# A graph-attention kernel: the row of target scores by a DRAM table and a broadcast load instead of TensorE transposes

## The chip, the cores and the metric

The kernel runs on one core of a Trainium2 chip. The core has TensorE (PE in the profile, its weight loads as PEld), VectorE (DVE), ScalarE (ACT), GpSimd (POOL) and SyncE (SP), which here issues nearly all ordinary transfers; sixteen DMA engines move the data. The metric is the device time of the whole kernel in microseconds, the median of several runs. One further execution was recorded by the hardware profiler, and all durations come from it.

## The reference

Four graph-attention layers run one after the other on 4096 nodes with 256 features. The adjacency matrix is 4096 × 4096, fixed and sparse, and denser towards the low node numbers. Layers 0 to 3 have 1, 1, 4 and 2 heads. (The two heads of layer 3 are the positive and the negative attention.) Each layer normalises the rows of x, projects them, scores every connected pair by a target part plus a source part, and takes the softmax over a target's sources. Cut to one layer with one head:

```python
h = jnp.maximum(_layernorm(x), 0.0) @ W
e = (h @ a1)[:, None] + (h @ a2)[None, :]      # target i, source j
e = jnp.where(e > 0, e, 0.2 * e)               # leaky relu
e = jnp.where(adj > 0, e, MASK_VAL)
x = x + elu(softmax(e, axis=1) @ h)
```

Layer 0 has a bias and no elu, layer 2 has four heads of 64 features and no elu, and layer 3 combines two attentions, the second with the signs of the scores turned, and returns the elu of their sum without adding x.

## The kernel before

The kernel uses that exp(leaky(s + t)) is the larger of exp(s + t) and exp(0.2(s + t)). With factors that cancel in the softmax taken out, the weight of source j for target i is max(grow[i], factor[j]) times the mask, where grow[i] = exp(0.8 s[i]). In layer 2 ScalarE makes two of the four heads of some units, in the form relu(grow · factor − 1), to be completed by VectorE; for these heads grow is the exp of −0.8 s. So everywhere one needs, for a block of targets, a tile in which every partition holds the same row: grow of these targets along the free dimension. How this row comes onto all partitions is what the change is about.

**Tiles and units.** The nodes are 32 tiles of 128. Per layer, `node_rows` (L683) normalises two tiles, transposes them (s_tp, L716), and calls `project` (L739), whose matmuls (s_pj, L748) give the features, two factors of the source, and the target score s. ScalarE writes the score of tile T to `L.s[:, T, :]` (L766 in layer 0, L773 in the others): one node per partition, one column per head. The features with their factors go to a DRAM table by SP (L727 in layer 0, four tiles at once; L729 in the others, each tile).

The attention itself is done by units (class `Unit`, L981). A dense unit holds four target tiles (512 targets) and runs over all 32 source tiles; there are 4, 2, 1 and 1 dense blocks in layers 0 to 3 (in layer 3 a block's two heads are two units that share their grow). A listed unit holds one target tile (128 targets) and runs over 4 source tiles kept in SBUF (pre) and then over 6 to 13 chunks of 128 sources from its own list, which GpSimd gathers from the DRAM table with an indirect transfer (s_gg, L1231). There are 16, 24, 28 and 28 listed units.

**grow.** `target_rows` (L954) makes it. For each head and target tile TensorE transposes the column of s, broadcast to 128 × 128, by the identity (s_sT, L967): the result in PSUM has the row of s on every partition. ScalarE takes the exp of it, scaled, into the SBUF tile s_grow (L973). The PSUM tiles come from a pool of two buffers that s_tp, s_pj and others share. For listed units and layer 0's dense units grow has two buffers; it is reused when the last weighing of the unit before the last is done.

**Order.** The steps of the units stand in a plan, and `run` (L1194) walks through it. At step p it fetches step p, begins step p−2 (ScalarE's relu in layer 2, L1019), weighs step p−3 (VectorE, L1033 and L1042, into s_p) and multiplies step p−6 (TensorE, s_acc at L1071, in layer 2 s_accm at L1096). Before these it prepares, that is makes grow of, a unit whose first step is four steps ahead, if all its scores are there:

```python
if p + 4 < n and plan[p + 4][1] == 0 and plan[p + 4][0].is_ready():
    plan[p + 4][0].prepare()
```

If they are not there yet, grow is made when the unit is first fetched. Between steps, parts of the work of finishing a tile and of projecting it for the next layer are pumped out of a queue by a clock of costs. In layer 0 the listed units are mixed with the dense steps, while the adjacency is loaded (s_raw, L1306, 512 KB each), turned into masks and stored. In layers 1 and 2 listed units are mixed with the dense steps until these are used up, and then follow each other alone; in layer 3 they run through all the dense steps. The program order is not final: a list scheduler reorders the instructions of TensorE, ScalarE, VectorE and SP. GpSimd keeps the written order. Each engine then runs its instructions in order, and so does SP, the queue of the stores and loads.

In layer 1 and later, some gathered rows carry the masks of the list along, which ScalarE copies out (mlist, L1056) ahead of their use.

The path through `list_layers` is the one that runs; `dense_layers` is a fallback behind a flag, and is not touched.

Of the kernel before, what the change touches and what calls it, by code (L numbers as in the profile page):

```python
# [8 lines left out]
F32 = mybir.dt.float32  # L9
# [3 lines left out]
AF = mybir.ActivationFunctionType  # L13
# [4 lines left out]
P = 128  # L18
N = 4096
# [7 lines left out]
SLOPE = 0.2  # L27
# [440 lines left out]
LH = (1, 1, HEADS, 2)  # L468
# [11 lines left out]
def list_layers(ctx: ExitStack, tc: tile.TileContext, a: dict, out: bass.AP, flag):  # L480

    nc = tc.nc
# [6 lines left out]
    dram = ctx.enter_context(tc.tile_pool(name="s_dram", bufs=1, space=bass.MemoryType.DRAM))  # L489
    ps_acc = ctx.enter_context(tc.tile_pool(name="s_acc", bufs=6, space=PSUM))  # L490
    ps_mm = ctx.enter_context(tc.tile_pool(name="s_mm", bufs=2, space=PSUM))


    ident = const.tile([P, P], F32, name="s_ident")
# [28 lines left out]
        if b not in MASKS_IN  # L523
    }

    def table_rows(t, jt):

        r0 = jt // CH * CH * P
        r0 += 1 if r0 >= HALF else 0
        return t[r0 : r0 + CH * P, :].rearrange("(p k) d -> p k d", k=CH)  # L530

    def feature_rows(l, jt):
        return table_rows(table[l], jt)[:, :, FRONT[l] : FRONT[l] + GW[l]]
# [149 lines left out]
    def node_rows(L, T0):  # L683


        u = f"{L.l}_{T0}"
        tiles = (T0, T0 + 1)
        while any(stored[T] < L.l - 1 for T in tiles) or not L.made:
            yield
        mv = small.tile([P, 2, 2], F32, name=f"s_mv_{u}", tag="mv")  # L690
        for k, T in enumerate(tiles):
            st6 = small.tile([P, 6], F32, name=f"s_st6_{u}_{k}", tag="st6")
            nc.vector.bn_stats(st6, x[:, T, :])
            nc.vector.bn_aggr(mv[:, k, :], st6)
            yield
        r = small.tile([P, 3, 2], F32, name=f"s_r_{u}", tag="r")
        nc.scalar.activation(r[:, 0], mv[:, :, 1], AF.Ln, bias=eps)
        nc.scalar.activation(r[:, 0], r[:, 0], AF.Exp, scale=-0.5)
        zs = []
        for k, T in enumerate(tiles):  # L700
            z = rows.tile([P, D], F32, name=f"s_z_{u}_{k}", tag="z", bufs=4)
            (nc.gpsimd if L.l == 0 else nc.vector).tensor_scalar(z, x[:, T, :], mv[:, k, 0:1], 0.0, op0=ALU.subtract, op1=ALU.max)
            zs.append(z)
        if L.bias is not None:
            for T in tiles:
                nc.gpsimd.tensor_add(x[:, T, :], x[:, T, :], L.bias[:, 0:D])
        yield 1.5

        nc.vector.scalar_tensor_tensor(r[:, 1], mv[:, :, 1], EPS, r[:, 0], op0=ALU.add, op1=ALU.mult)
        nc.vector.scalar_tensor_tensor(r[:, 1], r[:, 1], -0.5, r[:, 0], op0=ALU.mult, op1=ALU.mult)  # L710
        nc.vector.scalar_tensor_tensor(r[:, 2], r[:, 1], 1.5, r[:, 0], op0=ALU.add, op1=ALU.mult)
        hTs = []
        for k, T in enumerate(tiles):
            tp = ps_mm.tile([P, 2, P], F32, name=f"s_tp_{u}_{k}", tag="mm")
            for c in range(2):
                nc.tensor.transpose(tp[:, c, :], zs[k][:, c * P : (c + 1) * P], ident)  # L716
            hT = rows.tile([P, 2, P], F32, name=f"s_hT_{u}_{k}", tag="hT")
            nc.scalar.copy(hT, tp)  # L718
            hTs.append(hT)
            yield  # L720
        yield 1.5
        for k, T in enumerate(tiles):
            g = L.rows(T)
            yield from project(L, T, g, hTs[k], r[:, 2, k : k + 1])
            L.ready[T] = True
            if L.l == 0 and T % CH == CH - 1:
                nc.sync.dma_start(feature_rows(L.l, T), L.g[:, T - CH + 1 : T + 1, :])  # L727
            elif L.l > 0:
                nc.sync.dma_start(feature_rows(L.l, T)[:, T % CH, :], g)  # L729
# [9 lines left out]
    def project(L, T, g, hT, r):  # L739
        l, H, n = L.l, L.H, L.part  # L740
        u = f"{l}_{T}"
        re = small.tile([P, H], F32, name=f"s_re_{u}", tag=f"re{H}")
        parts = g.rearrange("p (h n) -> p h n", h=H)
        for k in range(2 if l == 3 else 1):
            cols = D if k else D + 3 * H
            ps = ps_mm.tile([P, cols], F32, name=f"s_pj_{u}_{k}", tag="mm")
            for c in range(2):
                nc.tensor.matmul(  # L748
                    ps,
                    lhsT=hT[:, c, :],  # L750
                    rhs=L.w[:, c, k * (D + 6) : k * (D + 6) + cols],
                    start=(c == 0),
                    stop=(c == 1),
                )
            if k == 0:
                t = ps[:, D + H : D + 3 * H]
                if L.bias is not None:
                    for i in range(2):
                        nc.scalar.activation(
                            g[:, D + i : D + i + 1],  # L760
                            t[:, i : i + 1],
                            AF.Exp,
                            scale=r,
                            bias=L.bias[:, D + 1 + i : D + 2 + i],
                        )
                    nc.scalar.activation(  # L766
                        L.s[:, T, :], ps[:, D : D + H], AF.Identity, scale=r, bias=L.bias[:, D : D + 1]
                    )
                else:
                    nc.scalar.activation(  # L770
                        parts[:, :, n - 2 : n], t.rearrange("p (h k) -> p h k", h=H), AF.Exp, scale=r
                    )
                    nc.scalar.activation(L.s[:, T, :], ps[:, D : D + H], AF.Copy, scale=r)  # L773
                nc.scalar.activation(re, parts[:, :, n - 2], AF.Copy, scale=r)
            if l == 2:
                nc.vector.tensor_tensor(
                    parts[:, :, 0:DH],
                    ps[:, 0:D].rearrange("p (h o) -> p h o", h=H),
                    re.unsqueeze(2).to_broadcast([P, H, DH]),
                    op=ALU.mult,  # L780
                )
            else:
                nc.scalar.activation(parts[:, k, 0:D], ps[:, 0:D], AF.Copy, scale=re[:, k : k + 1])
            yield
# [169 lines left out]
    def target_rows(L, T0, nt, big, nact):  # L954


        w = nt * P
        grow = (L.big if big else L.pool).tile(
            [P, L.H, w], F32, name=f"s_grow_{L.l}_{T0}", tag=big or "grow", bufs=None if big == "growb" else 2
        )  # L960
        per = max(1, 512 // w)
        for h0 in range(0, L.H, per):
            hs = range(h0, min(L.H, h0 + per))
            ps = ps_mm.tile([P, len(hs), nt, P], F32, name=f"s_sT_{L.l}_{T0}_{h0}", tag="mm")
            for h in hs:
                for it in range(nt):
                    nc.tensor.transpose(  # L967
                        ps[:, h - h0, it, :], L.s[:, T0 + it, h : h + 1].to_broadcast([P, P]), ident
                    )
            cut = min(max(L.H - nact, hs.start), hs.stop)  # L970
            for h1, h2, scale in ((hs.start, cut, 1.0 - SLOPE), (cut, hs.stop, SLOPE - 1.0)):
                if h1 < h2:
                    nc.scalar.activation(  # L973
                        grow[:, h1:h2, :],
                        ps[:, h1 - h0 : h2 - h0].rearrange("p h a b -> p h (a b)"),
                        AF.Exp,
                        scale=scale,
                    )
        return grow

    class Unit:  # L981
# [212 lines left out]
    def run(plan):  # L1194

        n = len(plan)
        for p in range(n + LEAD[3]):
            if p + 4 < n and plan[p + 4][1] == 0 and plan[p + 4][0].is_ready():
                plan[p + 4][0].prepare()
            for lead, stage in zip(LEAD, (Unit.fetch, Unit.begin, Unit.weigh, Unit.multiply)):  # L1200
                if 0 <= p - lead < n:
                    stage(*plan[p - lead])
            if p >= LEAD[3]:
                u = plan[p - LEAD[3]][0]
                clock[0] += u.cost
                pump(posts, u.rates[0], width=2)
                pump(lists_q, u.rates[1])
                gather_masks(u.rates[2])
# [39 lines left out]
    with ExitStack() as phase:  # L1248
# [130 lines left out]
        plan, listed = [], []  # L1379
# [3 lines left out]
        for ib in range(DENSE[0]):  # L1383
            for step in block(ib).plan():
                plan.append(step)
                if ib * NT + step[1] >= LISTED0:
                    n = 1 + step[1] % 2
# [12 lines left out]
    for l in (2, 3):  # L1400
        L = weights(l, late, late, nc.sync)
# [10 lines left out]
    plan = []  # L1412
    for l in (1, 2, 3):
        L = layers[l]
# [40 lines left out]
        else:  # L1455
            per = L.H
            first = []
            for ib in range(DENSE[l]):
# [8 lines left out]
                    per=per,  # L1467
# [78 lines left out]
```

## Time and profile before

| | us |
|---|---|
| median of 3 runs | 1781.22 |
| lowest and highest | 1780.12, 1788.01 |
| the profiled execution | 1697.57 |
| its span | 1695.8 |
| PE busy | 1619.6 |
| DVE busy | 1321.9 |
| POOL busy | 959.8 |
| ACT busy | 632.6 |

The profiled execution was shorter than the timed runs; sums over its records are to be held against its own time. The span runs from its first to its last record. The granted TensorE clock in it was 0.986 of full speed. A busy time counts the records of an engine, which for TensorE's pipelined matmuls is more than the time from one to the next. The DMA engines moved 274.70 MB. By the records, layer 0 takes until about 440 us, layer 1 until about 780, layer 2 until about 1275, and layer 3 the rest.

### The profile page before, as it was taken

The page shows a single profiled execution, that of the slowest core. Times are in us where ns is not written, and L with a number is a line of the kernel's source. Part 1 is how long each engine was busy: PE and PEld are TensorE (multiplying, and loading weights), DVE is VectorE, ACT ScalarE, POOL GpSimd, SP SyncE. Part 2 cuts the span into 40 slices and gives each one's busy share as a digit, 9 for nine tenths or more (in the row PEclk, how much of TensorE's full clock was granted, in tenths as well). Part 3 has the DMA queues.
Part 4 walks back from the last instruction along what each step waited for, and adds up shares of the span by engine and source line. Part 5 has one row for each costly group of instructions (what it writes and reads, how often), then busy time and mean ns, then how long its engine had stood idle before and what let it go on. Part 6 is the DMA issues. An engine that isn't in the chain of part 4 may idle for free.

```text
span 1695.8 us, 29208 instructions
## 1 busy us (share of the span) xinstructions
PE 1619.6 (96%) x9268; PEld 1366.4 (81%) x9268; DVE 1321.9 (78%) x3908; ACT 632.6 (37%) x1915; POOL 959.8 (57%) x930
## 2 busy tenths in 40 slices
PE   6999999899989999879999999999999999999997
PEld 4887778788868887766787787899988888888886
DVE  6888999888845786558898988988884777777765
ACT  5631010120211232333667766899991111111111
POOL 9836766757635766651555444445652655555463
PEclk9999999999989999989999999999999999999998
DMA  8899879954364545452333333333434666666554
GB/s 270 281 326 291 277 231 273 309 155 124 76 170 129 151 131 165 138 149 67 92 97 96 89 86 99 86 100 95 132 106 125 204 187 180 178 184 173 171 169 118
DMA packets 152237, 274.70 MB, mean 162 GB/s; under 512 B 21423, under 2 KB 75340, under 8 KB 152076
## 3 DMA queue, kind: packets, MB, share of 16 engines
q0 software_dynamic: 45584, 130.39, 28.7%
q1 hardware_dynamic: 105656, 141.83, 26.0%
q8 instruction: 77, 1.26, 0.3%
q14 instruction: 84, 0.69, 0.1%
q10 hardware_dynamic: 836, 0.53, 0.1%
HBM read 231.76 MB, written 40.90 MB: 161 GB/s over the span
## 4 chain that ended last, share of the span: by engine, by line
PE 52%; DMA 2%; DVE 1%; ACT 1%; issue 0%; POOL 0%; ACTq 0%; DVEq 0%; POOLq 0%
PE s_acc L1071 24%; PE s_accm L1096 22%; PE s_pj L748 3%; DMA s_gg<-table,idx 2%; PE s_sT L967 1%; PE s_tp L716 1%; PE s_oT L1158 0%; ACT s_p L1019 0%; DVE s_p L1033 0%; ACT mlist L1056 0%; DMA out<-s_out 0%; DVE s_p L1042 0%; POOL s_gg L1231 0%; DVE s_y L1187 0%; DVE s_out L1138 0%
## 5 line engine op out<-in xcount | busy, mean ns | idle before, releaser
L1231 POOL DMA_INDIRECT s_gg<-table,idx x715 | 751.7, 1051 | 643.8 <-PE s_acc L1071 219.4
L1033 DVE SCALAR_TENSOR_TENSOR s_p<-s_grow,s_gg,mlist 128x128 f32<-128x128 f32 x994 | 316.3, 349 | 103.1 <-PE s_acc L1071 55.3
L1071 PE MATMUL s_acc<-s_gg,s_p 128*128 128x257 f32 x1430 | 348.1, 387 | 6.3 <-DVE s_p L1033 6.3
L1071 PEld LDWEIGHTS s_acc<-s_gg,s_p 128*128 128x128 f32 x1430 | 268.0, 192 | 47.9 <-DVE s_p L1033 11.5
L1071 PE MATMUL s_acc<-g,s_p 128*128 128x257 f32 x1152 | 283.4, 387 | 13.2 <-DVE s_p L1033 9.1
L1071 PEld LDWEIGHTS s_acc<-g,s_p 128*128 128x128 f32 x1152 | 214.0, 192 | 46.9 <-DVE s_p L1033 14.7
L1033 DVE SCALAR_TENSOR_TENSOR s_p<-s_grow,pre,mpre 128x128 f32<-128x128 f32 (+1 forms) x576 | 191.1, 371 | 39.3 <-PE s_acc L1071 31.9
L1096 PE MATMUL s_accm<-s_p,s_gg 128*65 128x128 f32 x1744 | 204.0, 273 | 0.0
L1071 PE MATMUL s_acc<-s_gs,s_p 128*128 128x257 f32 x896 | 203.7, 380 | 0.0
L1033 DVE SCALAR_TENSOR_TENSOR s_p<-s_grow,s_gs,s_ms 128x512 f32<-128x512 f32 x224 | 162.6, 752 | 48.0 <-PE s_acc L1071 23.1
L1096 PEld LDWEIGHTS s_accm<-s_p,s_gg 128*65 128x65 f32 x1744 | 193.1, 138 | 2.5
L1019 ACT ACTIVATE s_p<-s_grow,s_minus,s_gg 128x128 f32<-128x128 f32 x436 | 186.6, 486 | 13.4 <-PE s_accm L1096 7.9
L1071 PEld LDWEIGHTS s_acc<-s_gs,s_p 128*128 128x128 f32 x896 | 169.4, 190 | 25.1 <-DVE s_p L1033 1.1
L1071 PE MATMUL s_acc<-pre,s_p 128*128 128x257 f32 x768 | 181.6, 381 | 0.0
L973 ACT ACTIVATE s_grow<-s_sT 128x256 f32<-128x256 f32 (+2 forms) x136 | 46.7, 367 | 346.9 <-PE s_sT L967 310.8
L748 PE MATMUL s_pj<-s_w,s_hT 128*128 128x259 f32 (+3 forms) x640 | 165.3, 399 | 8.4 <-ACT s_hT L718 4.4
L1071 PEld LDWEIGHTS s_acc<-pre,s_p 128*128 128x128 f32 x768 | 143.5, 191 | 20.9 <-PE s_acc L1071 0.3
L929 POOL DMA_INDIRECT mlist<-mask_t,idx x105 | 123.9, 1180 | 61.8 <-issue 29.1
L748 PEld LDWEIGHTS s_pj<-s_w,s_hT 128*128 128x128 f32 x640 | 122.2, 198 | 33.7 <-ACT s_hT L718 8.4
L1096 PE MATMUL s_accm<-s_p,pre 128*65 128x128 f32 (+1 forms) x928 | 119.6, 284 | 0.0
L1096 PEld LDWEIGHTS s_accm<-s_p,pre 128*65 128x65 f32 x928 | 103.6, 138 | 16.6 <-issue 14.0
L1019 ACT ACTIVATE s_p<-s_grow,s_minus,pre 128x128 f32<-128x128 f32 x224 | 96.4, 487 | 19.1 <-issue 11.6
(126 smaller groups left out, 1741.0 us busy)
## 6 DMA issues: line engine op xcount, KB each, us to landing
s_raw<-in_adjT SPq DMA_DIRECT2D x128, 512.0 KB
s_gs<-table SPq DMA_DIRECT2D x28, 516.0 KB
s_gg<-table,idx POOLq DMA_INDIRECT x715, 3.6
mask_t<-s_m SPq DMA_DIRECT2D x35, 256.0 KB
table<-s_g SPq DMA_DIRECT2D x28, 258.0 KB
s_ms<-mask_t SPq DMA_DIRECT2D x28, 256.0 KB
table<-s_m SPq DMA_DIRECT2D x21, 256.0 KB
table<-g SPq DMA_DIRECT2D x8, 516.0 KB
```

What stands on the lines that cost most here:

```text
L716: nc.tensor.transpose(tp[:, c, :], zs[k][:, c * P : (c + 1) * P], ident)
L748: nc.tensor.matmul(ps, lhsT=hT[:, c, :], rhs=L.w[:, c, k * (D + 6) : k * (D + 6) + cols], start=(c == 0), stop=(c == 1),)
L929: nc.gpsimd.indirect_dma_start(out=mlist[:, OFFS[T] + k, :], out_offset=None, in_=mask_t[T // IT], in_offset=bass.IndirectOffsetOnAxis(ap= ...
L967: nc.tensor.transpose(ps[:, h - h0, it, :], L.s[:, T0 + it, h : h + 1].to_broadcast([P, P]), ident)
L973: nc.scalar.activation(grow[:, h1:h2, :], ps[:, h1 - h0 : h2 - h0].rearrange("p h a b -> p h (a b)"), AF.Exp, scale=scale,)
L1019: nc.scalar.activation(w[:, h, :], u.grow[:, h, :], AF.Relu, scale=g[h][:, n - 1 : n], bias=minus)
L1033: nc.vector.scalar_tensor_tensor(p[:, k, :], u.grow[:, h, :], g[k][:, n - 1 : n], m, op0=ALU.min if L.l == 3 and h == 1 else ALU.max, op1= ...
L1071: nc.tensor.matmul(u.accs[it][h], lhsT=p[:, k, it * P : (it + 1) * P], rhs=g[k][:, 0:n], start=first, stop=last,)
L1096: nc.tensor.matmul(u.regions[h], lhsT=g[k][:, 0 : DH + 1], rhs=p[:, k, :],  start=first and (u.nt > 1 or h == 0), stop=last, skip_group_ch ...
L1231: nc.gpsimd.indirect_dma_start(out=wide, out_offset=None, in_=L.table, in_offset=bass.IndirectOffsetOnAxis(ap=index[T][:, k : k + 1], axis=0),
```

## The change

The target scores take another way to the row. There is one small DRAM table per layer, `s_rows`, with a row of 4096 scores for every head. After a tile is projected, SP stores its column (or columns) of s there, element by element, ahead of the store of the features. `target_rows` then loads the wanted piece of the table with one transfer that repeats it on all 128 partitions, straight into grow, and ScalarE takes the exp in place. The 256 transposes and their PSUM tiles are gone; 128 stores and 104 loads are new. The exps of all heads with one scale are now one instruction. A unit is prepared eight steps ahead instead of four.

```diff
+    s_rows = [dram.tile([LH[l], N], F32, name=f"s_rows{l}", tag=f"s_rows{l}") for l in range(4)]
...
             yield from project(L, T, g, hTs[k], r[:, 2, k : k + 1])
+            nc.sync.dma_start(s_rows[L.l][:, T * P : (T + 1) * P].rearrange("h p -> p h"), L.s[:, T, :])
             L.ready[T] = True
...
-        per = max(1, 512 // w)
-        for h0 in range(0, L.H, per):
-            hs = range(h0, min(L.H, h0 + per))
-            ps = ps_mm.tile([P, len(hs), nt, P], F32, name=f"s_sT_{L.l}_{T0}_{h0}", tag="mm")
-            for h in hs:
-                for it in range(nt):
-                    nc.tensor.transpose(
-                        ps[:, h - h0, it, :], L.s[:, T0 + it, h : h + 1].to_broadcast([P, P]), ident
-                    )
-            cut = min(max(L.H - nact, hs.start), hs.stop)
-            for h1, h2, scale in ((hs.start, cut, 1.0 - SLOPE), (cut, hs.stop, SLOPE - 1.0)):
-                if h1 < h2:
-                    nc.scalar.activation(
-                        grow[:, h1:h2, :],
-                        ps[:, h1 - h0 : h2 - h0].rearrange("p h a b -> p h (a b)"),
-                        AF.Exp,
-                        scale=scale,
-                    )
+        nc.sync.dma_start(
+            grow, s_rows[L.l][:, T0 * P : T0 * P + w].unsqueeze(0).to_broadcast([P, L.H, w])
+        )
+        cut = L.H - nact
+        for h1, h2, scale in ((0, cut, 1.0 - SLOPE), (cut, L.H, SLOPE - 1.0)):
+            if h1 < h2:
+                nc.scalar.activation(grow[:, h1:h2, :], grow[:, h1:h2, :], AF.Exp, scale=scale)
         return grow
...
-            if p + 4 < n and plan[p + 4][1] == 0 and plan[p + 4][0].is_ready():
-                plan[p + 4][0].prepare()
+            if p + 8 < n and plan[p + 8][1] == 0 and plan[p + 8][0].is_ready():
+                plan[p + 8][0].prepare()
```

## The prediction

> **What bounds the kernel now.** I first read the busy shares and the slices, then the shares of the chain that ended last:
>
> ```profile
> PE 1619.6 (96%) x9268; PEld 1366.4 (81%) x9268; DVE 1321.9 (78%) x3908; ACT 632.6 (37%) x1915; POOL 959.8 (57%) x930
> ...
> PE   6999999899989999879999999999999999999997
> ...
> PE 52%; DMA 2%; DVE 1%; ACT 1%; issue 0%; POOL 0%; ACTq 0%; DVEq 0%; POOLq 0%
> ```
>
> TensorE is busy nearly everywhere and owns almost all of the chain that the profile could follow. The exceptions are the first slice and the slices near 720 us, between layers 1 and 2. What TensorE no longer has to do should therefore shorten the span, unless another engine is nearly full in the same stage. The table by windows (PE, PEld, DVE, ACT, POOL busy, clock, DMA share, GB/s) shows where that is so:
>
> ```profile
> 100.00:200.00 100.00, 92.20 (x567) 77.86 (x566) 88.07 (x188) 10.68 (x39) 61.00 (x51) 0.98 0.91 295
> ...
> 1100.00:1200.00 100.00, 99.64 (x829) 95.44 (x828) 87.89 (x319) 94.20 (x266) 53.43 (x49) 1.00 0.35 99
> ...
> 1400.00:1500.00 100.00, 100.00 (x469) 87.17 (x468) 73.95 (x230) 13.70 (x35) 57.82 (x59) 1.00 0.61 179
> ```
>
> Layer 0 (first row) has busy DMA and DVE beside TensorE. Late layer 2 has ACT at 94%. Layer 3 has TensorE alone. The groups by shape and the chain in order of time (start, duration, piece) price the transposes:
>
> ```profile
> L967 PE MATMUL s_sT<-s_ident,s_s x256: 271/272/473, 26.5 to 1658.3; 128*128 128x128 f32 x128
> ```
> ```profile
> 812.27 0.44 PE s_sT L967 x4
> 1055.22 0.55 PE s_sT L967 x4
> ```
> ```profile
> ACT s_grow L973 <- PE s_sT L967: 310.8, 74, 28.0
> ```
>
> One transpose record lasts 272 ns, but four in a full stream take 0.44 to 0.55 us, that is 0.109 to 0.137 us each. The 310.8 us that ACT waits for them is no cost: ACT has nothing else to do there.
>
> **What the Trainium skill says.** "TensorE: Matmul & The Clock Gate", Part 4, PE-mode transpose: a transpose is a matmul whose output lands in PSUM, about 275 ns in one kernel. The record agrees (272 ns); the pitch in the stream is smaller, and the pitch counts. "DMA: Bandwidth & Descriptors", Anatomy of one DMA: some 2.0 us of a transfer are fixed, mostly the receipt of the last write, and waits for semaphores are served on the issuing sequencer, not in the DMA engines. The nearest row here, a 128 KB store of the output, has 2.82 us in the chain (`1687.00 2.82 DMA out<-s_out`), which fits. The same page, Specifications, says that below 512 B a DMA write becomes a read-modify-write, and its rules for kernel authors that a non-contiguous last dimension becomes one descriptor per element. The new stores are of that kind; the trace of before has no such store.
>
> **The change part by part**, against the profiled execution (1697.57 us, span 1695.8). The median of the timed runs is 1781.22, 1.049 times as much; I scale the sum by that.
>
> *Removed: 256 transposes* (32, 32, 128 and 64 in layers 0 to 3). At 0.109 us: 27.9 us; at 0.137: 35. I take 27.9. By layer: 3.5, 3.5, 14.0, 7.0. Of layer 2's 14.0, 44 transposes (4.8 us) belong to the 11 listed units that run from 1100 to 1270 us without dense work between them (the profile has 22 exps there, two a unit). The exps stay: 136 become 132, reading SBUF where they read PSUM. At 367 ns, four fewer save 1.5 us of ACT: nothing on the path.
>
> *Added: 128 stores of s and 104 loads, all on SP.* At 0.34 us an issue, as for the table stores near 28 us, this is 79 us of SP in 1696; SP waits for work most of its time, so it costs nothing by itself. In order, though, a store of s that waits for ACT's s stops the raw adjacency loads and tables behind it. The loads write 64 KB per head and tile, 16.8 MB against 274.70 MB in all, 6%. Small beside a DMA share of 0.35 to 0.61 in layers 2 and 3, not beside 0.91 in layer 0.
>
> *One load on its way*: 0.4 us issue and some 3 us to landing (estimate from the output store's 2.82 us for 128 KB). In layer 0 it also stands behind loads of 512 KB, which take 1.8 us each at 295 GB/s. The store ahead is unknown: if its 128 to 512 elements of 4 B cost like other small packets it adds under 0.5 us, and if each is slow several us. Mostly it is issued long before its load is due, so I take nothing, except at the start.
>
> *Start.* Now the first exp runs at 27.55 and the first attention matmul at 30.48. The first unit needs s of tile 3 (written at 26.61 to 26.97), then a store to DRAM, its receipt, the load behind a table store of 516 KB and a raw load, then the exp: about 2.5 + 3.5 + 1.8 + 0.6 us after 27.0, that is 35.4 for the end of the exp, against 28.1 now: 7 us later. TensorE can project later tiles meanwhile (8 matmuls in 2.02 us at 28.63). I take +4, bounds 0 and +8.
>
> *Layer 0.* Preparing eight steps ahead instead of four covers the 3.5 us of a load many times. But stores of s hold back SP's raw loads while DMA is 0.91 busy, and DVE, at 88%, waits on that data. I take +3, which eats this layer's 3.5; bounds 0 and +7.
>
> *Layers 1 to 2.* Between 700 and 800 us TensorE is idle for 15 us, waiting for own gathers and ACT's mask copies (L1056). Exps that wait for a DMA now stand in ACT's order between those copies. +2, bounds 0 and +5. The rest of layer 1 keeps its 3.5.
>
> *Layer 2, early units.* There are two grow buffers, so the load for unit k+1 can be issued only when DVE has finished unit k−1, and its exp follows on ACT right after. ACT then waits some 3.5 us, with the Relu weights of unit k queued behind it. Between listed units lie six or seven dense steps (about 5.8 us of TensorE) and ACT is 70 to 75% busy: covered, 0. Without that cover it would be 3.5 us for each of 17 units.
>
> *Layer 2, late units.* ACT has no such room: over 1100 to 1270 us it is busy 94.20 + 65.71 = 159.9 of 170, so 10 us are free. The exp for unit k+1 stands one to four steps of 1.1 us into unit k, so that between none and all of the 3.5 us is left; I take a third, 1.2, as the mean wait. 11 × 1.2 − 10 = +3.2, and, as ACT then sets the pace, TensorE's 4.8 us are not gained: +8.0.
>
> *Layer 3.* The load goes out after unit k's last weighing, the exp falls in ACT's gaps of 5 to 6 us (the timeline shows 5.55 us ahead of one exp), and TensorE is at 100%: all of the 7.0.
>
> *Sum*: −27.9 + 4 + 3 + 2 + 8.0 = −10.9 us of the profiled execution; times 1.049 it is −11.4, so 1781.2 − 11.4 = about 1770 us.
>
> **The rivals.** (a) *ACT's wait in late layer 2 replaces the transposes.* Only its 0.34 us issue and 3 us flight are needed. For it: 94% busy, in order, two buffers, so loading early is impossible however early the unit is prepared. Against: the scheduler puts the exp later than the load. With all 3.5 us uncovered: 11 × 3.5 − 10 = 28.5; the net is −18.9 (the other terms) + 4.8 + 28.5 = +14.4, scaled 15.1: about 1796 us. It decides from the point where −18.9 + 4.8 + 11x − 10 is zero, at x = 2.2 us of mean wait. (b) *The whole gain comes through*: the start hidden by projections, ACT's waits inside its slack. −27.9 to −35, scaled 1752 to 1744. For it: TensorE at 96%, and the exps have DMA-sized gaps in three layers; against it the 10 us of late layer 2. (c) *Nothing is left*: start +8, layer 0 +7, boundary +5, late layer 2 +8.0 give +28 against −27.9: 1781. For it: DMA at 0.91 and a new round trip through DRAM ahead of the first unit. That the transposes remain somewhere is excluded: the code has no other path to grow.
>
> **How the numbers follow.** The likeliest case, 1763 to 1776, has 0.46; (a) 0.19; (b) 0.13; (c), 1776 to 1788, 0.19; something unseen, such as stores of single elements that clog the queues, 0.03. A change of 0.5% is 8.9 us, about what a measurement can tell: faster means under 1772.3. Of the likeliest case some three quarters are faster (0.36), the rest the same. With (b) that is 0.49, and 0.02 from edges of other cases: 0.51. The same: 0.10 of the likeliest, 0.14 of (c), none else: 0.24. Slower: (a), 0.04 of (c) and the unseen: 0.25. The range of 1746 to 1802 leaves out a part of (b), the far side of (a) (a flight longer than 3 us) and most of the unseen, under 2 in 10 together.
>
> **What would show it.** TensorE without L967, its busy time some 46 us lower in records; stage by stage, layer 3 shorter by about 7 us and layer 2 from 1100 on no shorter. The first attention matmul near 38 us. In the waits, ACT's exp waiting on the DMA of grow: long totals in layers 0, 1 and 3 with nothing behind them, and about 1 us per late unit of layer 2, with TensorE waiting for s_p there. A mean wait near 3 us would make (a) true. I would also be wrong if the stores of s took several us to land, if SP held back the tables of sources behind them, or if layer 0 lost its pace for want of raw loads.

## The result and the profile after

The changed kernel takes 2324.53 us (median of 4 runs), the kernel before beside it 1782.37. The ratio is 1.302, with a 95% interval of 1.297 to 1.307: 30% slower, where 0.6% less was forecast and 1802 us was the end of the range. The profiled execution took 2321.85 us, its span is 2320.1. (The kernel before takes 1782 to 1800 us on some chips and about 1700 on others, so times are compared as ratios to its runs on the same chip; its own trace is of an execution of 1697.57 us, and the 1.049 by which the prediction scaled was of that size too.)

First the busy shares, the slices, the DMA packets and the chain's shares of the profile page after:

```profile
PE 1761.0 (76%) x9012; PEld 1433.6 (62%) x9012; DVE 1312.4 (57%) x3908; ACT 623.5 (27%) x1911; POOL 924.6 (40%) x930
...
PE   4857787889877565565768779686665798999997
...
DMA  8999989866577889778663556345564556666654
GB/s 184 176 171 219 251 190 222 220 120 134 69 148 108 88 65 85 90 94 93 82 37 88 73 83 76 68 90 69 74 67 66 100 74 184 213 189 187 196 161 125
DMA packets 216878, 291.61 MB, mean 126 GB/s; under 512 B 57903, under 2 KB 138444, under 8 KB 216716
...
PE 37%; DMA 35%; issue 10%; DVE 10%; ACT 5%; POOL 1%; SPq 1%; another core or an unknown queue 1%; ACTq 0%; DVEq 0%; POOLq 0%
```

TensorE no longer owns the chain: its share fell from 52% to 37%, and DMA rose from 2% to 35%. The two DMA rows together say what kind of trouble this is. In layer 1 (slices from about 660 to 1145 us) the sixteen engines are six to nine tenths busy while they move under 100 GB/s much of the time. They are occupied and move little. Now the table by windows (PE, PEld, DVE, ACT, POOL busy, clock, DMA share, GB/s), one row of each layer:

```profile
100.00:200.00 100.00, 58.37 (x265) 47.43 (x265) 45.70 (x99) 18.73 (x65) 20.80 (x20) 0.76 0.94 162
...
1000.00:1100.00 100.00, 55.48 (x198) 42.14 (x198) 32.18 (x102) 20.27 (x78) 38.77 (x39) 0.72 0.83 94
...
1700.00:1800.00 100.00, 63.64 (x451) 58.70 (x449) 49.21 (x178) 51.71 (x148) 28.05 (x28) 0.80 0.56 67
...
2100.00:2200.00 100.00, 100.00 (x462) 87.32 (x462) 72.45 (x230) 13.56 (x36) 54.97 (x55) 1.00 0.65 194
```

Only layer 3, in which no score is stored, runs with TensorE at 100% as before. The granted clock of TensorE fell too: it is 0.76, 0.72, 0.80 and 1.00 in these rows, and 0.868 in the whole against 0.986. It is low in the rows in which TensorE is busy only 55 to 64% of the time. The attention multiplies of layer 0 that read g last 423 ns on average instead of 387, and TensorE's busy time rose from 1619.6 to 1761.0 us although 256 transposes are gone. No run changes the clock alone, so how much of the loss goes through it is not known.

Lengths of the layers, read from the timelines (layer 0 from the start of the span, each to the first attention multiply of the next, layer 2 to its last, layer 3 from there to the end of the span; by this count layer 0 lasts longer than the 440 us given ahead of the prediction):

| us | layer 0 | layer 1 | layer 2 | layer 3 |
|---|---|---|---|---|
| before | 487 | 296 | 493 | 420 |
| e4, in place of before on a slower chip | 530 | 316 | 524 | 429 |
| after | 660 | 485 | 737 | 438 |

The trace of before was taken at the faster pace, that of after where the kernel before takes 1782 us. So the second row is the fairer one to hold the third against: it is the kernel before with additions that cost it 0.5% (the experiment e4 below), where the kernel before takes 1800 us.

The chain in order of time has the new stores on it, and the new loads:

```profile
24.09 9.52 DMA s_rows<-s_s
...
864.43 21.55 DMA s_rows<-s_s
...
1321.15 16.60 DMA s_grow<-s_rows
```

The first is a store of 128 elements (512 bytes), the second one of 512 elements, the third a load of 256 KB. What such stores do to all else shows in the DMA view of the window from 24.5 to 33.5 us, in 40 slices of 0.225 us each:

```profile
DMA  0103993900019900398909040090005899999999
GB/s 0 9 0 55 73 36 27 9 9 9 0 18 18 36 0 0 18 18 36 27 9 73 0 18 0 0 55 18 0 18 182 346 419 401 382 391 382 339 448 375
```

Before, the same view from 18 to 38 us (slices of 0.5 us) has four slices in a row without data at most:

```profile
GB/s 389 385 377 156 8 213 188 336 283 37 0 61 238 233 311 197 8 0 0 0 0 405 363 291 150 248 213 299 406 356 354 373 381 406 401 385 180 53 4 330
```

For 30 slices, some 6.7 us, little arrives after the change, although SP has loads of 512 KB in its queue; after that the rate is at once 350 to 450 GB/s. Two stores of s were issued shortly before the window, at 19.42 and 21.19 us, and two more at 24.09 and 25.36. The packet records tell which of them hold the engines: the packets of the first two stores stand at 20.3 and 22.2 us, with 9 ns each, and no further packet of 4 bytes comes before 31.5 us. So this stretch follows on the 256 elements of the first two stores, and the third store itself waits in it. The last of its 16 landing marks in the trace comes at 40.2, 16 us after its issue (the chain leaves it at an earlier mark, after 9.52). The cost does not appear as long packets of the stores. It appears in what comes after them: single packets of 2048 bytes, which otherwise take 84 ns, take up to 4.0 us in this window. Over the whole execution 3425 packets take over 1 us, against 205 before, and together they hold an engine for 550 us on average, against 16. The gathers of GpSimd, which have a queue of their own, are hit as well: 1281 of their queue's packets take over 1 us, against 113.

The first unit starts late for this reason:

```profile
45.86 0.63 ACT L970 ACTIVATE s_grow<-s_grow 128x512 f32<-128x512 f32 x1 [13.04 <-DMA s_grow<-s_rows]
```

The bracket is the time for which ACT stood idle ahead of it and what ended it. This exp stood at 27.55 before, and the first attention multiply comes at 47.40 where it came at 30.48.

### The profile page after: what moved, and what is told of

It reads as the page before. It is cut to its first block, busy times and chain, and to the rows that moved or that the text cites. A ratio compares the mean times of both kernels' runs of the same rounds, so it can differ in the third digit from the quotient of the medians.

```text
span 2320.1 us, 29071 instructions
## 1 busy us (share of the span) xinstructions
PE 1761.0 (76%) x9012; PEld 1433.6 (62%) x9012; DVE 1312.4 (57%) x3908; ACT 623.5 (27%) x1911; POOL 924.6 (40%) x930
## 3 DMA queue, kind: packets, MB, share of 16 engines
q1 hardware_dynamic: 170296, 158.75, 40.2%
## 4 chain that ended last, share of the span: by engine, by line
PE 37%; DMA 35%; issue 10%; DVE 10%; ACT 5%; POOL 1%; SPq 1%; another core or an unknown queue 1%; ACTq 0%; DVEq 0%; POOLq 0%
PE s_acc L1063 26%; DMA s_gg<-table,idx 11%; DMA s_grow<-s_rows 11%; PE s_accm L1088 6%; DMA s_raw<-in_adjT 6%; DVE s_p L1025 4%; PE s_pj L751 3%; ACT s_p L1011 2%; DMA table<-s_g 2%; DMA s_rows<-s_s 2%; PE idx_ps L903 1%; DMA mask_t<-s_m 1%; DVE s_p L1034 1%; DVE s_m L1317 1%; POOL s_gg L1223 1%
## 5 line engine op out<-in xcount | busy, mean ns | idle before, releaser
L1063 PE MATMUL s_acc<-s_gg,s_p 128*128 128x257 f32 x1430 | 378.3, 407 | 140.2 <-DVE s_p L1025 129.1
L1063 PE MATMUL s_acc<-g,s_p 128*128 128x257 f32 x1152 | 317.2, 423 | 72.5 <-DVE s_p L1025 56.6
L970 ACT ACTIVATE s_grow<-s_grow 128x256 f32<-128x256 f32 (+3 forms) x132 | 51.5, 406 | 1035.1 <-DMA s_grow<-s_rows 822.5
L1063 PEld LDWEIGHTS s_acc<-g,s_p 128*128 128x128 f32 x1152 | 237.4, 213 | 119.3 <-DVE s_p L1025 64.4
L751 PE MATMUL s_pj<-s_w,s_hT 128*128 128x259 f32 (+3 forms) x640 | 188.3, 440 | 64.2 <-ACT s_g L786 33.4
L1088 PE MATMUL s_accm<-s_p,s_gg 128*65 128x128 f32 x1744 | 219.5, 284 | 18.5 <-issue 12.8
L1088 PEld LDWEIGHTS s_accm<-s_p,s_gg 128*65 128x65 f32 x1744 | 206.8, 145 | 26.7 <-issue 15.4
L1025 DVE SCALAR_TENSOR_TENSOR s_p<-s_grow,pre,mpre 128x128 f32<-128x128 f32 (+1 forms) x576 | 188.5, 367 | 61.1 <-PE s_acc L1063 29.5
L751 PEld LDWEIGHTS s_pj<-s_w,s_hT 128*128 128x128 f32 x640 | 136.1, 220 | 98.7 <-ACT s_g L786 36.0
L1088 PE MATMUL s_accm<-s_p,pre 128*65 128x128 f32 (+1 forms) x928 | 133.6, 303 | 37.1 <-DVE s_p L1034 33.1
L1317 DVE TENSOR_SCALAR s_m<-s_raw 128x1024 uint8<-128x1024 int32 x112 | 78.4, 716 | 123.4 <-DMA s_raw<-in_adjT 120.9
```

The costliest lines, as they stand in the source:

```text
L751: nc.tensor.matmul(ps, lhsT=hT[:, c, :], rhs=L.w[:, c, k * (D + 6) : k * (D + 6) + cols], start=(c == 0), stop=(c == 1),)
L970: nc.scalar.activation(grow[:, h1:h2, :], grow[:, h1:h2, :], AF.Exp, scale=scale)
L1025: nc.vector.scalar_tensor_tensor(p[:, k, :], u.grow[:, h, :], g[k][:, n - 1 : n], m, op0=ALU.min if L.l == 3 and h == 1 else ALU.max, op1= ...
L1063: nc.tensor.matmul(u.accs[it][h], lhsT=p[:, k, it * P : (it + 1) * P], rhs=g[k][:, 0:n], start=first, stop=last,)
L1088: nc.tensor.matmul(u.regions[h], lhsT=g[k][:, 0 : DH + 1], rhs=p[:, k, :],  start=first and (u.nt > 1 or h == 0), stop=last, skip_group_ch ...
L1317: nc.vector.tensor_scalar(m[:, h * half : (h + 1) * half, :], raw, 0.0, None, op0=ALU.is_gt)
```

## The experiments

**Stores alone, loads alone.** The change has two halves that can be had one without the other.

e1, stores only, is the kernel before and the store:

```diff
             yield from project(L, T, g, hTs[k], r[:, 2, k : k + 1])
+            nc.sync.dma_start(s_rows[L.l][:, T * P : (T + 1) * P].rearrange("h p -> p h"), L.s[:, T, :])
```

> The kernel before, with the 128 stores of s to the DRAM tables added and nobody reading them; transposes and exps stay, units are prepared four steps ahead. Theory (the element-wise stores clog the DMA engines: in the changed kernel the first one held the engines for some 6.5 us and one of 512 elements stood for 21.55 us on the chain): most of the loss is here, 2200 to 2330 us, and layer 3, in which no score is stored, keeps its 410 us. Rival (the loss comes from the loads of grow and from ACT and SP waiting in order for them): 1781 to 1800 us.

Measured: 2231.22 us, ratio 1.240 (1.228 to 1.253). Its layers take 662, 493, 650 and 437 us: layers 0 and 1 are as long as in the changed kernel (660 and 485). So the stores, which nobody reads here, are enough for these two layers' whole loss. In layer 2 they cost 126 us against e4, where the changed kernel loses 213.

e2, loads only, is the changed kernel with

```diff
-            nc.sync.dma_start(s_rows[L.l][:, T * P : (T + 1) * P].rearrange("h p -> p h"), L.s[:, T, :])
...
-            grow, s_rows[L.l][:, T0 * P : T0 * P + w].unsqueeze(0).to_broadcast([P, L.H, w])
+            grow,
+            a["x"].rearrange("(h a) d -> h (a d)", h=16)[0 : L.H, T0 * P : T0 * P + w].unsqueeze(0).to_broadcast([P, L.H, w]),
```

> The changed kernel without its stores of s and without the table: the same 104 broadcast loads, of the same size and at the same places, read rows of the input x instead (so the scores are not those of the graph; the work is the same). Theory (stores): close to the kernel before, 1755 to 1785 us, that is what was predicted for the change. Rival (loads and the waits for them): 2200 us or more.

Measured: 1783.82 us, ratio 0.989 (0.986 to 0.992). The loads at this place are no disaster, and neither is SP's waiting in order for them. This kernel also leaves out the round trip of the first scores through DRAM, so it flatters layer 0.

**What is slow about the stores.** e3 and e4 add as many stores at the same places in SP's order to the kernel before, with another target:

```diff
+    s_rows = [dram.tile([LH[l], N, P], F32, name=f"s_rows{l}", tag=f"s_rows{l}") for l in range(4)]
...
+            nc.sync.dma_start(s_rows[L.l][:, T * P : (T + 1) * P, 0].rearrange("h p -> p h"), L.s[:, T, :])
```

and for e4, in place of the last line,

```diff
+            nc.sync.dma_start(
+                s_rows[L.l][:, T * P : (T + 1) * P, :].rearrange("h p d -> p h d"),
+                g[:, 0:P].unsqueeze(1).to_broadcast([P, L.H, P]),
+            )
```

> As stores only, but each of the 4-byte elements goes to its own 512 bytes of DRAM. If small writes wait for each other because neighbours share a piece of DRAM (128 elements took 6.5 us, some 50 ns each, which looks like a queue at one place), this is 1785 to 1830 us. If every small write is slow by itself on its engine (8 in a row, 0.8 us each), it is as slow as stores only, 2200 to 2330 us.

> As stores spread, but each of the stores writes 512 bytes (features instead of scores, 128 times as much data), the same number of instructions and pieces on the same queue. Theory (writes under 512 bytes are slow): 1785 to 1830 us, the 16.8 MB more being 6% of all traffic. Rival (the number of pieces, or the store's place in SP's order ahead of loads, is what costs): as slow as stores only, 2200 us or more.

Measured: 1.012 (1.004 to 1.020) for 4-byte elements 512 bytes apart, 1.005 (1.002 to 1.008) for pieces of 512 bytes. The number of pieces, their size of 4 bytes, the issue on SP and the store's place in its order all stay in e3, and 23 of the 24% are gone. What is left is that the elements are neighbours in DRAM. e7 and e12 change the distance alone (the last dimension of the table is 16 or 4 elements instead of 128):

> Stores spread, but 64 bytes apart instead of 512. If writes wait for each other only within one piece of 64 bytes, this is like stores spread (ratio 1.01). If the piece is larger, up to 512 bytes, it is in between or as slow as stores only (1.24).

> Stores spread, with the 4-byte elements 16 bytes apart: four instead of sixteen share 64 bytes. If what counts is that 64 bytes are shared at all, this is as slow as stores only (ratio 1.20 to 1.26). If the cost grows with the number of elements in a piece, it is in between (1.02 to 1.15). If pieces of 16 bytes are already apart, it is like the stores 64 bytes apart (1.005 to 1.012).

Measured: 1.008 (1.005 to 1.011) at 64 bytes and 1.025 (1.020 to 1.030) at 16 bytes. So with 4-byte elements at distances of 4, 16, 64 and 512 bytes the ratios are 1.240, 1.025, 1.008 and 1.012. The cost is that of elements written close together, and it grows the closer they lie. Packets over 1 us number 3687 in stores only, 920 at 16 bytes, 207 at 64 bytes, 462 at 512 (e3, on a slower chip) and 205 before. The first store of each kernel shows it alone: from its issue to its last landing mark the 128 elements take 8.4 us as neighbours, 2.2 at 16 bytes, 1.5 at 64 and 1.4 at 512. (The expectations of e1 and e3 speak of 6.5 us for one store of 128 elements in the changed kernel. That was the window above, which has two stores ahead of it; alone, the first one took 7.8 us there.) That the writes wait for each other at the memory is what these numbers look like. The trace does not show the memory's side, so this mechanism is argued, not shown, and so is 64 bytes as the size of a shared piece: wider tables are also spread over more of the DRAM.

**What is slow about the loads.** e5 was meant as a repair: in layers 2 and 3 one transpose per tile gives a row of 128 scores per head, which is stored whole.

```diff
+            if L.l >= 2:
+                st = ps_mm.tile([L.H, P], F32, name=f"s_st_{u}_{k}", tag="mm")
+                nc.tensor.transpose(st, L.s[:, T, :], ident)
...
+                if L.l == 2:
+                    nc.scalar.copy(row, st)
+                else:
+                    nc.vector.tensor_copy(row, st)
+                nc.sync.dma_start(s_rows[L.l][:, T * P : (T + 1) * P], row)
```

> A version that keeps the loads and drops the element-wise stores: in layers 2 and 3 each tile's scores are transposed once on TensorE ([128 x heads] to [heads x 128]), copied to SBUF (by ACT in layer 2, by DVE in layer 3) and stored as pieces of 512 bytes; grow is loaded from there as in the changed kernel, eight steps ahead. Layers 0 and 1 stay as before. It issues 64 transposes where there were 192, so 128 x 0.109 = 14 us of TensorE less, with some given back in late layer 2 as in loads only. Theory (only stores of single neighbouring elements are harmful): ratio to the kernel before 0.990 to 1.000. Rival (any store of scores ahead of the loads costs some per cent): 1.02 or more.

Measured: 1.112 (1.109 to 1.115), far from the 0.990 to 1.000 of the theory. Layer 0 keeps its 487 us, layer 1 takes 312, and layer 2 grows to 661. The chain of this kernel in layer 2 has a load of grow for every unit:

```profile
1190.43 8.27 DMA s_grow<-s_rows
1213.49 8.56 DMA s_grow<-s_rows
1235.05 8.49 DMA s_grow<-s_rows
```

They are 7.9 to 9.2 us in 22 of 25 cases on the chain of layer 2. In loads only (e2) the loads on the chain there take 3.4 to 4.3 us. The form of the load is the same, 512 packets of 512 bytes; the rows of the four heads lie 16 KB apart in the table and 256 KB apart in x. e11 changes that distance alone in loads only (`a=16` in place of `h=16`); e9 lays e5's table out tile by tile, so that the heads of a tile are one piece (each partition then reads one packet of 2 KB where it read four of 512 bytes):

> Loads only with the rows of the heads 16 KB apart in x, as in the table of scores, instead of 256 KB. If the distance of the heads' rows makes the loads slow (8.2 to 9.2 us in layer 2), layer 2 slows down as in row23: ratio 1.08 to 1.12. If it is something else about the table (its place, or that it was just written): like loads only, 0.985 to 1.005.

> As row23, but the table of scores is laid out tile by tile, so that the scores of all heads of a tile are one piece (2 KB in layer 2, 1 KB in layer 3) instead of pieces of 512 bytes 16 KB apart. In row23 a load of layer 2's grow took 8.2 to 9.2 us on the chain, against 3.4 to 4.4 in loads only, where the pieces of the heads lie 256 KB apart, and TensorE fell to 77% in layer 2. Theory (pieces of 512 bytes 16 KB apart, read by all partitions at once, are what made row23 slow): loads of some 3 to 4 us and a ratio of 0.990 to 1.005. Rival (a row read by all partitions from the small table, or a row that was just written, is slow in any layout): 1.05 to 1.11.

Measured: e11 1.055 (1.053 to 1.058), e9 1.015 (1.012 to 1.017); each lies between the two cases of its expectation. The chains of e11, of e9 and of e10 (loads only once more, below), in this order, one kernel a fence:

```profile
1116.04 6.82 DMA s_grow<-in_x
1135.33 6.56 DMA s_grow<-in_x
1155.30 6.50 DMA s_grow<-in_x
```
```profile
1111.22 3.34 DMA s_grow<-s_rows
1126.72 3.24 DMA s_grow<-s_rows
```
```profile
1176.98 3.21 DMA s_grow<-in_x
1188.72 3.85 DMA s_grow<-in_x
```

With the rows 16 KB apart a load mostly takes 6.3 to 7.6 us (23 of 25 on the chain of layer 2) instead of 3.2 to 4.2, and layer 2 takes 582 us instead of 495. All other layers stay within 3 us of e10's. So the distance of the heads' rows costs. With the rows in one piece the loads are short again, 3.0 to 4.4 us, though the table was just written; e9 changes the size of the packets with the distance, so which of the two did it is not separated there. Why the table of e5 is slower still (7.9 to 9.2 us) than the same distance in x stays open.

**The sum.** Stores only adds 24.0%, loads at 16 KB 5.5%, together 29.5% of the 30.2%. In layer 2 it comes out alike: 126 us by the stores (e1 against e4) and 87 by the loads (e11 against e10), 213 together, and 213 in the changed kernel against e4. That the sum closes is partly luck. The loads of the changed kernel read the table, as those of e5 do, and e5's layer 2 is 157 us longer than that of e9, which differs from it in the layout of the table. 126 and 157 are more than 213: if the loads alone cost as much here, the two losses overlap, and what each has of layer 2 is not settled. That the stores are the larger part of the whole is.

**Eight steps instead of four.** e6 is loads only with four steps, e8 the kernel before with eight, e10 repeats e2:

> Loads only, with a unit prepared four steps ahead instead of eight (the scores are again rows of x). Theory (the two grow buffers, not the place of the preparation, set when a load can go out): within 0.5% of loads only, so a ratio of 0.985 to 0.995 to the kernel before. Rival (the early preparation hides the load): 1.00 or more.

> The kernel before with its units prepared eight steps ahead instead of four and nothing else changed. It should make no difference: ratio 0.995 to 1.005. Its profile serves to compare stages with that of loads only.

> Loads only once more (grow loaded from rows of x, no stores, eight steps ahead), because the first gave 0.989 where the kernel before took 1800 us and the variant with four steps 1.003 where it took 1699 us. If the number of steps makes the difference: 0.985 to 0.995 again. If it is the chip on which it runs: 1.000 to 1.005 where the kernel before takes about 1700 us.

Measured: e6 1.003 (1.002 to 1.005), e8 1.005 (1.004 to 1.006), e10 1.003 (1.002 to 1.005). e6 missed its theory (0.985 to 0.995), but e10 gives the same ratio with eight steps: for loads the number of steps makes no difference that shows. For the kernel with transposes eight steps cost half a per cent. The e10 result also says that loads without any store are no gain where the kernel before takes 1700 us.

**Where the price of the transposes went.** Without the stores the 27.9 us of the transposes should have come out as gain, less what the loads cost; in e10 nothing came. e13 leaves the row out (the exp reads the identity, so grow has no scores in it), e14 writes each transpose twice, e15 is loads only beside them:

```diff
-                    nc.tensor.transpose(
-                        ps[:, h - h0, it, :], L.s[:, T0 + it, h : h + 1].to_broadcast([P, P]), ident
-                    )
+                    for _ in range(2):
+                        nc.tensor.transpose(
+                            ps[:, h - h0, it, :], L.s[:, T0 + it, h : h + 1].to_broadcast([P, P]), ident
+                        )
```

(This is e14; e13 has only the lines taken out.)

> The kernel before without the 256 transposes and with nothing in their place: the exps take a constant tile instead of the row of scores (so grow does not hold the graph's values), no stores, no loads, four steps ahead. It tells what the transposes are worth on the path. As predicted, 27.9 us or 1.6%: ratio 0.982 to 0.986. If TensorE's time is only partly the limit where they stand (ACT in late layer 2, DVE and DMA in layer 0): 0.988 to 0.996.

> The kernel before with each of the 256 transposes done twice, into the same place. The price of a transpose from the other side: 256 x 0.109 = 27.9 us gives a ratio of 1.016; 1.004 to 1.012 if part of it falls into time in which TensorE waits anyway.

> Loads only again, to stand on one chip beside the kernel without rows. It gave 0.989 on a chip on which the kernel before took 1800 us, and 1.003 where it took 1699. With the price of the transposes known from the run beside it, the difference is what the loads and the waits for them cost: as predicted 15 to 19 us (1%) of 27.9; if they cost all that the transposes did, the ratio is again 1.000 to 1.005.

Measured: 0.988 (0.984 to 0.992), 1.013 (1.010 to 1.016) and 0.998 (0.995 to 1.002). The kernel before took 1785.16 us there, so the transposes are worth 21 us when taken away (14 to 28 by the interval) and 23 when added (17 to 28), some 0.085 us each. Loads only keeps about 3 us of these 21 (by its interval, between a gain of 10 and a loss of 3): the loads give most of it back even without the stores. Loads only has thus measured 0.989, 1.003 and 0.998; what makes it differ between chips was not found. Where it gives back can be seen in late layer 2, in the table by windows of e8 (first fence) and of e10 (second), and in ACT's waits of e10 between 1090 and 1290 us:

```profile
1090.00:1200.00 110.00, 109.50 (x925) 105.55 (x924) 98.00 (x359) 105.08 (x304) 54.69 (x52) 1.00 0.34 98
1200.00:1290.00 90.00, 84.37 (x702) 80.66 (x701) 75.71 (x254) 76.60 (x232) 48.25 (x45) 1.00 0.40 110
```
```profile
1090.00:1200.00 110.00, 104.27 (x854) 97.49 (x853) 92.55 (x340) 99.61 (x291) 52.74 (x50) 1.00 0.42 119
1200.00:1290.00 90.00, 82.85 (x698) 79.64 (x697) 77.63 (x269) 80.34 (x245) 49.81 (x48) 1.00 0.46 127
```
```profile
ACT s_grow L969 <- DMA s_grow<-in_x: 10.3, 9, 1.9
```

TensorE is busy 104.27 + 82.85 = 187.1 us in e10, against 193.9 in e8 (109.50 + 84.37), and the stretch is no shorter: what TensorE saves, it waits.

No version that beats the kernel before came out of this. An elementwise store into SBUF instead of DRAM was not tried on the chip.

## Why the prediction was wrong

**The store of s, the step that failed.** The prediction said: "The store ahead is unknown: if its 128 to 512 elements of 4 B cost like other small packets it adds under 0.5 us, and if each is slow several us. Mostly it is issued long before its load is due, so I take nothing, except at the start." Both halves were wrong. The size: the first store of 128 elements took 7.8 us from issue to landing, the third 16, and one of 512 elements stood on the chain for 21.55. And the kind of cost: it was weighed as a delay of the one load that needs the row, which time ahead can hide, and not as time in which the sixteen engines move little for anyone. So beside 2.5 us at the start and the 3 of layer 0 nothing stood in the sum for the stores, and e1 shows that they cost 24%. Had "several us" been multiplied by 128 stores, the upper bound alone would have been several hundred us; in the forecast, stores that "clog the queues" had 0.03. Of the two rules of the Trainium skill that were cited there from "DMA: Bandwidth & Descriptors", the one under Rules for kernel authors agrees with the trace: the kernel with the stores has one 4-byte packet for each of the 32768 elements. The other, under Specifications (writes under 512 bytes are read-modify-writes), is not supported as the price: 4-byte stores 64 bytes apart cost 0.8%. The same page has under Back-pressure in remote DMA, for another case, that stalled writes also stall an engine's other queues; here the 1281 long packets of GpSimd's queue, against 113 before, agree with it.

**One load on its way**, 3 us: right for rows 256 KB apart or in one piece (3.0 to 4.4), wrong for this table (7.9 to 9.2 in layer 2 of e5, up to 18.5 behind stores in the changed kernel). An estimate from a store's time says nothing of where the pieces of a load lie. (The 2.0 us of fixed cost that the prediction quoted stand in the page's section on transfers that GpSimd issues; these are issued by SP.) The rival (a) named 2.2 us of mean wait in late layer 2 as the point from which ACT's waits decide. In late layer 2 of e11 ACT waits 46.3 us in 12 waits for its loads, so e11 is past that point, and it lost 5.5%, more than the rival's 1796 us. With loads of that length the range would have been missed even without the stores.

**The transposes**, 27.9 us: the mechanism held, the measured size is 21 to 23, and 27.9 lies at the end of both intervals. If it was too much, the likely reason is that the pitch of a full stream was charged for all of them, also where TensorE waits anyway; this is not shown. (The page's 275 ns, which the record's 272 were said to agree with, are of a bf16 transpose; these are fp32.)

**Start**: the first attention multiply near 38 us was forecast, 47.40 measured. The order of events was right. The load of the first row could go out only when the fourth store had landed, and SP stood still for it for 13.4 us:

```profile
40.51 0.32 SPq L964 DMA_DIRECT2D s_grow<-s_rows  x1
```

That is 15 us after the issue of this store at 25.36, where 2.5 were taken.

**Layer 0**, +3: it lost 131 us against e4 (173 against the trace of before, which is of the faster pace), and as much with the stores alone. The prediction did say that stores of s could hold back layer 0's raw loads; the reason given, SP's order, was not it, since e3 and e4 keep that order and cost 1.2% at most.

**Late layer 2**: for loads alone the size came out: from the last dense step to the end of layer 2 e10 takes 198.3 us and e8 195.3, so 3.0 us more where +3.2 was worked out. Partly this was luck. The mean wait is 8.5 / 11 = 0.8 us where 1.2 was taken (8.5 of the 10.3 us above fall before the layer's end), and by the prediction's own sum 8.5 us would have fitted into the 10 us that ACT has free.

**Early layer 2**, 0, also held in e10 for loads of 3 us: 297.0 us from the first multiply of the layer to its last dense step, against 298.9 in e8, but this is not the 9 us of gain that the transposes there were credited with: 2 us came. With the longer loads of e11 it did not hold: 335.7 us.

**Layer 3**: all of the 7.0 was expected; its attention took 405.7 us in e10 against 408.4 in e8, so 2.7 of it came. Another 3.0 us went where TensorE waits twice for ACT's s_y, both times shortly after a load of grow on the chain (4.77 us at 1329, 4.43 at 1639).

**Eight steps ahead** was given no cost. With transposes it costs 0.5% (e8).

## What to carry to other kernels

In this kernel, DMAs that scattered 4-byte elements next to each other in DRAM had to be priced by the time for which they hold up all other transfers, times their count, and not by their latency; time ahead did not hide them. Writing such a column as whole pieces, or keeping the elements 64 bytes apart, cost under 1% here. When the trace has no example of a new kind of transfer, its upper bound has to go into the sum once for every time that it runs.

## What the runs showed of the hardware

- 4-byte stores to DRAM, 32768 of them in 128 transfers: ratio 1.240 when they are neighbours, 1.025 at 16 bytes, 1.008 at 64, 1.012 at 512. In pieces of 512 bytes: 1.005.
- The packets of such stores are recorded with 9 ns each. What follows is held up: after two stores of 128 neighbouring elements, other packets of 2048 bytes take up to 4.0 us instead of 84 ns.
- The first store of 128 elements lands 8.4 us after its issue when they are neighbours, 2.2 at 16 bytes, 1.5 at 64, 1.4 at 512.
- A broadcast of four rows of 512 bytes to 128 partitions takes 3.2 to 4.3 us with the rows 256 KB apart and mostly 6.3 to 7.6 with the rows 16 KB apart. With the rows in one piece it takes 3.0 to 4.4.
- A transpose of 128 × 128 in fp32 is worth some 0.085 us in this kernel (0.06 to 0.11 by the intervals); its pitch in a full stream is 0.109.
